# The fourth channel block of a convolutional feed-forward: one product of 128 channels, or four of 32

## The chip, the cores and the metric

The kernel runs on one core of one Trainium2 chip. The metric is the device time of one execution in microseconds (us); runs of the kernel before have a median of 4023.7 us.

## The reference

One block of an image-restoration network, in float32, on `x` of 16 images, 128 channels, 96 x 96 pixels. It is channel attention with a residual, then a feed-forward network with a residual:

```python
xn1 = _layernorm(x_hwc, ln1_w, ln1_b)              # over the 128 channels of a pixel
x = x + _attention(xn1, wq, wk, wv, wp)            # 8 heads; attends between channels, 16 x 16 a head
xn2 = _layernorm(x_hwc, ln2_w, ln2_b)
h1 = jnp.einsum('bchw,oc->bohw', xn2, w_in)        # 128 -> 512 channels, the first projection
h2 = depthwise 3 x 3 convolution of h1 with w_dw   # each of the 512 channels by itself, zeros around
h3 = jax.nn.gelu(h2, approximate=False)
x = x + jnp.einsum('bchw,oc->bohw', h3, w_out)     # 512 -> 128 channels
```

## The kernel before

Channels lie on the 128 partitions and pixels on the free axis. An image is cut into 6 bands of 16 rows (`BR`), so there are 96 bands (`NG`), and the 512 hidden channels into four blocks of 128 (`n` from 0 to 3, the fourth is `PE_CHUNK`). The normalized image lies in `ring`, a buffer of 124 rows that wraps around.

For a band `g` and a block `n`, `conv_job` works in these steps:

- `hidden` (L953): TensorE (PE in the profile) multiplies a chunk of four or five rows, 384 or 480 pixels, by the first projection, into one of four PSUM banks (`H_BANKS`). Where the chunk's rows wrap around in the ring, `pieces` cuts them and there are two products.
- `kept` (L956): ScalarE (ACT) copies the chunk to SBUF and adds the bias.
- `product` (L976) and `add_products` (L990): two of the nine taps of the convolution are made by ScalarE and added by DMAs that GpSimd (POOL) issues.
- `tap` (L983): VectorE (DVE) does the other seven taps, one instruction for each.
- `gelu` (L994): ScalarE applies the activation. Then `ffn_out` (L1083) multiplies by the second projection on TensorE, four rows at a time, four blocks into one bank.

The fourth block has two ways. In some bands (`by_pe(g)`, about three of seven) its projection and its convolution are one set of nine products on TensorE, `by_matmuls` (L1048), and no `conv_job` is made. In the other bands it goes through `conv_job` like the other blocks. A chunk of the fourth block begins two rows later where the band above was a `conv_job` too, as those rows are copied over from it (`halo`).

Around this, TensorE transposes tiles for both normalizations (L695, L781), forms the attention's channel products (L747) and applies the attention's matrix (L644). The attention's small steps are on TensorE in L837 to L919.

The order of all work is made before the program is: `Plan` is a list scheduler with a duration for each operation, four PSUM banks and the other buffers as resources, and a place in line (`AT`, `STEP`) for each kind. The order that it gives is the order on each engine's queue; the hardware only waits where data or a buffer isn't there. `hidden` is handed to it as one operation with the duration `t_mm((e - r) * W)`:

```python
pe(t_mm((e - r) * W), at("hidden", jk, g >= HEAD), lambda r=r, e=e: hidden(r, e), [*zs, ("w", "in")], [ph])
```

Of the kernel before, what the change touches and what calls it, by code (L numbers as in the profile page):

```python
# [21 lines left out]
PE_CHUNK = 3  # L22
# [217 lines left out]
def tile_restormer_block(  # L240
# [24 lines left out]
    nc = tc.nc  # L265
    B, C, H, W = x.shape
    P = 128
# [57 lines left out]
    winT = const.tile([P, NCH, P], F32, name="winT")  # L325
# [26 lines left out]
    def pieces(i, r, n):  # L352

        out, done = [], 0
        while done < n:
            at_ = (i * H + r + done) % RING
            m = min(n - done, RING - at_)
            out.append((done, m, ring[:, at_ : at_ + m, :]))
            done += m
        return out  # L360
# [7 lines left out]
    def rows(t):  # L368
        return t.rearrange("p (r w) -> p r w", w=W)
# [17 lines left out]
    def bank(key, n=4 * P):  # L387

        return banks[plan.slot["h", key]][:, :n]
# [542 lines left out]
    def conv_job(j, g, n):  # L932
# [17 lines left out]
        def hidden(r, e):  # L950
            ph = d["ph", r] = bank((jn, r), (e - r) * W)
            for k, m, z in pieces(i, r0 - 1 + r, e - r):
                nc.tensor.matmul(rows(ph)[:, k : k + m, :], lhsT=winT[:, n, :], rhs=z, start=True, stop=True)  # L953

        def kept(r, e):
            nc.scalar.activation(  # L956
# [44 lines left out]
        for k, (r, e) in enumerate(chunks):  # L1001
            ph = ("h", (jn, r))
            jk, zs = j + STEP["hidden"] * k, z_units(i, r0 - 1 + r, r0 - 1 + e)
            to = [("h1", n, k)]
            if r < 2:
                to.append(("h1", n, "first"))
            if e > BR:
                to.append(("h1", n, "last"))
            pe(t_mm((e - r) * W), at("hidden", jk, g >= HEAD), lambda r=r, e=e: hidden(r, e), [*zs, ("w", "in")], [ph])
            act(t_act((e - r) * W, 1) - 43, at("kept", jk, g >= HEAD), lambda r=r, e=e: kept(r, e), [ph], to)  # L1010
# [177 lines left out]
```

## Time and profile before

| | |
|---|---|
| median of the runs | 4023.7 us (4021.5 to 4025.9) |
| profiled execution, from its first to its last instruction | 4032.2 us |
| instructions | 51,195 |
| PE (products) busy | 3973.7 us, 99% |
| DVE busy | 3964.5 us, 98% |
| ACT busy | 3704.6 us, 92% |
| POOL busy | 1939.2 us, 48% |
| PE weight loads busy | 2593.8 us, 64% |

The profiled execution has no time of its own beside its span, which is 0.2% above the median of the runs. PE's row in the profile counts the products, PEld the weight loads, which run beside them. A line of a group reads: code line, engine, operation, tile written <- tiles read, shapes, number; then busy us, mean ns of one, idle us of the engine ahead of it and what ended that. For a matmul, "128*128" is rows (input channels) by columns (output channels) of the weights, and "128x384" the pixels that pass by. A line of the timeline reads: start, length (both us), engine, line, operation, tiles, shape, number of instructions merged.

### The profile page before, as it was taken

The numbers are of one execution on the slowest core, as the hardware profiler recorded it, in microseconds if no ns is written. First come the engines' busy times: TensorE is split into PE (matmuls) and PEld (weight loads), VectorE is DVE, ScalarE is ACT, GpSimd is POOL, SyncE is SP. The second block draws the span as 40 slices with busy tenths as digits, with TensorE's granted clock in tenths as the row PEclk, the third lists the DMA queues.
The fourth block names the chain that finished last, engine by engine and source line by source line (L and its number), as shares of the span: only waits on it lengthen the run. The fifth ranks groups of instructions, "written<-read, shape, count | busy, mean of one in ns | idle before, by whom it ended". The sixth has DMA issues, their size and how long they took to land.

```text
span 4032.2 us, 51195 instructions
## 1 busy us (share of the span) xinstructions
PE 3973.7 (99%) x17048; PEld 2593.8 (64%) x17048; DVE 3964.5 (98%) x3478; ACT 3704.6 (92%) x7676; POOL 1939.2 (48%) x1596
## 2 busy tenths in 40 slices
PE   9999999999999999999999999999999999999989
PEld 7666666666666666666666666666666666666555
DVE  6999999999999999999999999999999999999999
ACT  7999999899999999999999999999999999999985
POOL 4545445454554544545455454544545455454431
PEclk9999999999999999999999999999999999999999
DMA  5999999999999999999999999999999999999997
GB/s 143 211 202 208 195 218 217 193 230 197 216 220 208 216 203 223 213 209 215 203 215 213 202 216 195 233 206 209 227 196 215 214 219 219 205 214 187 202 192 156
DMA packets 197159, 834.19 MB, mean 207 GB/s; under 512 B 22816, under 2 KB 24352, under 8 KB 196896
## 3 DMA queue, kind: packets, MB, share of 16 engines
q0 software_dynamic: 138960, 679.10, 85.9%
q1 hardware_dynamic: 57936, 151.83, 10.4%
q8 instruction: 136, 2.23, 0.2%
q14 instruction: 127, 1.04, 0.1%
HBM read 150.62 MB, written 149.42 MB: 74 GB/s over the span
## 4 chain that ended last, share of the span: by engine, by line
PE 75%; DVE 11%; ACT 8%; DMA 2%; issue 2%; POOL 2%; POOLq 0%; DVEq 0%; ACTq 0%; SPq 0%
PE h L1083 19%; PE h L1048 19%; PE h L953 16%; DVE h L983 10%; PE g L747 6%; PE h L644 4%; PE pB_a L781 3%; PE pT_a L695 3%; PE pB_b L781 2%; PE pT_b L695 2%; ACT h L976 2%; ACT h L956 1%; POOL rstd_b L713 1%; ACT zT L738 1%; DMA x<-in_x_dram 1%
## 5 line engine op out<-in xcount | busy, mean ns | idle before, releaser
L983 DVE SCALAR_TENSOR_TENSOR h<-h,ratio,h 128x1520 f32<-128x1520 f32 (+1 forms) x1712 | 2983.7, 1778 | 6.5
L1083 PE MATMUL h<-h,woutT 128*128 128x384 f32 x3072 | 1131.9, 488 | 4.1 <-ACT h L956 3.6
L976 ACT ACTIVATE h<-h,ratio 128x1536 f32<-128x1536 f32 (+1 forms) x682 | 1090.3, 1610 | 5.6 <-PE h L1083 3.8
L1048 PE MATMUL h<-xn,comp 128*128 128x380 f32 (+5 forms) x3090 | 1074.7, 478 | 4.4 <-ACT h L956 3.7
L953 PE MATMUL h<-xn,winT 128*128 128x384 f32 (+3 forms) x2720 | 1065.5, 494 | 8.6 <-ACT h L956 4.7
L990 POOL DMA_DIRECT2D h<-h x682 | 628.7, 957 | 885.2 <-ACT h L976 399.5
L956 ACT ACTIVATE h<-h,beta 128x384 f32<-128x384 f32 (+1 forms) x1318 | 791.2, 632 | 76.9 <-PE h L953 54.8
L1083 PEld LDWEIGHTS h<-h,woutT 128*128 128x128 f32 x3072 | 554.2, 190 | 335.0 <-issue 36.7
L1048 PEld LDWEIGHTS h<-xn,comp 128*128 128x128 f32 x3090 | 557.2, 191 | 312.5 <-issue 22.2
L713 POOL TENSOR_TENSOR rstd_a<-ve_a,mhalf 128x4 f32<-128x4 f32 x288 | 527.5, 1844 | 447.1 <-ACT ve_a L709 428.0
L713 POOL TENSOR_TENSOR rstd_b<-ve_b,mhalf 128x4 f32<-128x4 f32 x288 | 564.6, 1986 | 351.4 <-ACT ve_b L709 346.2
L953 PEld LDWEIGHTS h<-xn,winT 128*128 128x128 f32 x2720 | 486.1, 190 | 279.8 <-issue 19.8
L983 DVE SCALAR_TENSOR_TENSOR h<-h,ratio 128x1536 f32<-128x1536 f32 x342 | 618.4, 1810 | 5.9 <-ACT h L956 3.2
L994 ACT ACTIVATE h<-h 128x1536 f32<-128x1536 f32 (+1 forms) x345 | 520.7, 1510 | 23.9 <-DMA h<-h 21.4
L738 ACT ACTIVATE zT<-pT_b,rstd_b 128x128 f32<-128x128 f32 x1132 | 329.6, 403 | 35.4 <-POOL rstd_b L713 33.4
L738 ACT ACTIVATE zT<-pT_a,rstd_a 128x128 f32<-128x128 f32 x1080 | 316.5, 411 | 4.8 <-POOL rstd_a L713 3.7
L747 PEld LDWEIGHTS g<-zT 128*128 128x128 f32 x2160 | 275.0, 191 | 42.8 <-ACT zT L738 0.9
L644 PE MATMUL h<-xn,mwT 128*128 128x384 f32 x768 | 296.2, 490 | 5.5 <-ACT h L1063 2.1
L656 POOL DMA_DIRECT2D x<-in_x_dram x189 | 182.1, 967 | 237.4 <-ACT x L653 166.6
L747 PE MATMUL g<-zT 128*128 128x129 f32 x2160 | 285.5, 274 | 0.3 <-ACT zT L738 0.3
L653 ACT ACTIVATE x<-h,d 128x384 f32<-128x384 f32 x378 | 227.1, 637 | 11.2 <-PE h L644 4.3
L781 PEld LDWEIGHTS pB_b<-ident,zT 128*128 128x128 f32 x1152 | 147.0, 142 | 111.0 <-issue 52.2
(185 smaller groups left out, 3226.3 us busy)
## 6 DMA issues: line engine op xcount, KB each, us to landing
h<-h POOLq DMA_DIRECT2D x569, 768.0 KB, 10.0
h<-h POOLq DMA_DIRECT2D x113, 720.0 KB, 13.2
x<-in_x_dram SPq DMA_DIRECT2D x192, 384.0 KB, 8.2
out_dram<-x SPq DMA_DIRECT2D x190, 384.0 KB, 9.9
x<-in_x_dram POOLq DMA_DIRECT2D x189, 384.0 KB, 10.7
out_dram<-h POOLq DMA_DIRECT2D x94, 768.0 KB, 10.3
out_dram<-x SPq DMA_DIRECT2D x4, 192.0 KB, 1.9
h<-in_L_conv_w_in_dram SPq DMA_DIRECT2D x1, 256.0 KB, 6.3
```

Source lines behind the costliest of these rows:

```text
L644: nc.tensor.matmul(rows(pm), lhsT=mats[i][0], rhs=interior(i, u), start=True, stop=True)
L713: nc.gpsimd.tensor_tensor(rstd, d["ve"], mhalf, ALU.pow)
L738: nc.scalar.activation(zT(q)[:, k, :P], d["pT", q][:, k, :], AF.Copy, scale=d["rstd"][:, t : t + 1])
L747: nc.tensor.matmul(grams[i][:, : P + 1], lhsT=zt[:, :P], rhs=zt, start=(q == 0 and k == 0), stop=(q == NU * TPU // QT - 1 and k == QT - 1),)
L953: nc.tensor.matmul(rows(ph)[:, k : k + m, :], lhsT=winT[:, n, :], rhs=z, start=True, stop=True)
L956: nc.scalar.activation(window(h1_, r, e - r, 1), rows(d.pop(("ph", r))), AF.Identity, bias=beta[:, n : n + 1])
L976: nc.scalar.activation(d["pr", t][:, o0:o1, :], shifted(t, o0, o1), AF.Copy, scale=ratio[:, n, t : t + 1])
L983: nc.vector.scalar_tensor_tensor(h3[:, o0:o1, w0:w1], shifted(t, o0, o1, w0, w1), ratio[:, n, t : t + 1], onto, ALU.mult, ALU.add)
L990: nc.gpsimd.dma_start(out=to[:, o0:o1, :], in_=d["pr", t][:, o0:o1, :], accum_op=ALU.add)
L994: nc.scalar.activation(h3, h3, AF.Gelu)
L1048: nc.tensor.matmul(d["pc"][:, o0 + k : o0 + k + m, w0:w1], lhsT=comp[:, t, :], rhs=z[:, :, w0 + dx : w1 + dx], start=(t == order[0]), stop ...
L1083: nc.tensor.matmul(rows(d["po"]), lhsT=woutT[:, n, :], rhs=h3s[g, n][:, s * UR : (s + 1) * UR, :], start=(k == 0), stop=(k == NCH - 1),)
```

## The change

In the products of `hidden`, where the block is the fourth, the 128 output channels are cut into four slices of 32. Each slice has a product of its own, with 32 columns of the weights, the same pixels, and 32 partitions of the same PSUM bank as its output. Blocks 0 to 2 keep one product. The planner's durations and places are as they were.

```diff
         def hidden(r, e):
             ph = d["ph", r] = bank((jn, r), (e - r) * W)
             for k, m, z in pieces(i, r0 - 1 + r, e - r):
-                nc.tensor.matmul(rows(ph)[:, k : k + m, :], lhsT=winT[:, n, :], rhs=z, start=True, stop=True)
+                parts = [slice(c, c + 32) for c in range(0, P, 32)] if n == PE_CHUNK else [slice(0, P)]
+                for c in parts:
+                    nc.tensor.matmul(
+                        rows(ph)[c, k : k + m, :], lhsT=winT[:, n, c], rhs=z, start=True, stop=True
+                    )
```

## The prediction

> **What bounds the kernel now.** I read the page first (busy shares, slices, the chain), then what TensorE (PE) waits for, then its instructions in order of time, to see how far apart two products start.
>
> ```profile
> PE 3973.7 (99%) x17048; PEld 2593.8 (64%) x17048; DVE 3964.5 (98%) x3478; ACT 3704.6 (92%) x7676; POOL 1939.2 (48%) x1596
> ...
> PE   9999999999999999999999999999999999999989
> ...
> PEclk9999999999999999999999999999999999999999
> ...
> PE 75%; DVE 11%; ACT 8%; DMA 2%; issue 2%; POOL 2%; POOLq 0%; DVEq 0%; ACTq 0%; SPq 0%
> ```
>
> PE is busy in every slice at a full clock and is 75% of the chain. DVE at 98% is nearly as full, ACT at 92% less. A busy PE can hide short stalls, because the recorded end of a product lies behind the start of the next one. So the next view gives PE's idle time, the first two and the last of 26 rows:
>
> ```profile
> PE pB_b L781 <- ACT xn L784: 8.6, 8, 2.7
> PE h L953 <- ACT h L956: 4.7, 7, 2.2
> ...
> PE pB_a L781 <- ACT zT L738: 0.2, 1, 0.2
> ```
>
> The 26 rows add up to 53 us, and 4032.2 - 3973.7 is 58.5 us. What PE could give back by waiting less is at most that. The timeline shows what its busy time consists of:
>
> ```profile
> 1999.72 1.77 PE L953 MATMUL h<-xn,winT 128*128 128x480 f32 x4
> 2001.50 5.43 PE L1083 MATMUL h<-h,woutT 128*128 128x384 f32 x16
> 2006.77 2.73 PE L1048 MATMUL h<-xn,comp 128*128 128x384 f32 x8
> 2009.33 0.60 PE L695 MATMUL pT_b<-ident,x 128*128 128x128 f32 x4
> ```
>
> and the groups, each shape apart, how many there are:
>
> ```profile
> L1083 PE MATMUL h<-h,woutT 128*128 128x384 f32 x3072 | 1131.9, 488 | 4.1 <-ACT h L956 3.6 <-ACT h L994 0.3
> ...
> L953 PE MATMUL h<-xn,winT 128*128 128x384 f32 x2060 | 800.4, 488 | 6.8 <-ACT h L956 4.3 <-ACT x L653 1.0 <-ACT h L1063 0.8
> L1048 PE MATMUL h<-xn,comp 128*128 128x380 f32 x1916 | 720.4, 484 | 0.0
> ...
> L983 DVE SCALAR_TENSOR_TENSOR h<-h,ratio 128x1536 f32<-128x1536 f32 x342 | 618.4, 1810 | 5.9 <-ACT h L956 3.2 <-PE h L1083 2.1 <-ACT zT L738 0.6
> ...
> L1048 PE MATMUL h<-xn,comp 128*128 128x384 f32 x958 | 391.7, 491 | 4.4 <-ACT h L956 3.7 <-ACT h L1063 0.8
> ...
> L644 PE MATMUL h<-xn,mwT 128*128 128x384 f32 x768 | 296.2, 490 | 5.5 <-ACT h L1063 2.1 <-ACT x L653 1.7 <-ACT h L956 1.2
> L747 PE MATMUL g<-zT 128*128 128x129 f32 x2160 | 285.5, 274 | 0.3 <-ACT zT L738 0.3
> ...
> L953 PE MATMUL h<-xn,winT 128*128 128x480 f32 x508 | 241.2, 567 | 1.2 <-ACT x L653 0.8 <-ACT h L956 0.4
> ...
> L781 PE MATMUL pB_b<-ident,zT 128*128 128x128 f32 x1152 | 191.3, 275 | 9.8 <-ACT xn L784 8.6 <-ACT zT L738 1.0
> ...
> L781 PE MATMUL pB_a<-ident,zT 128*128 128x128 f32 x1080 | 177.7, 273 | 0.2 <-ACT zT L738 0.2
> ...
> L695 PE MATMUL pT_b<-ident,x 128*128 128x128 f32 x1132 | 169.8, 274 | 5.1 <-ACT zT L738 2.5 <-DMA x<-in_x_dram 2.4
> L695 PE MATMUL pT_a<-ident,x 128*128 128x128 f32 x1080 | 162.3, 273 | 2.0 <-ACT zT L738 2.0
> ```
>
> Eight records of 384 columns last 2.73 us together and one lasts 0.491, so they start (2.73 - 0.49) / 7 = 0.320 us apart, not 0.49. In the same way records of 480 columns are (1.77 - 0.567) / 3 = 0.401 us apart, those of 128 (0.60 - 0.274) / 3 = 0.109. L1083 has 96 bands x 4 steps x 4 blocks = 1536 products in the code and 3072 records: one f32 product is two records, each with a weight load, so 384 columns cost 0.64 us. Now PE's real work: 6858 records of 384 columns at 0.320 (2195 us), 508 of 480 at 0.401 (204), 1916 of 380 at 0.317 (607), 2160 of 129 and 4444 of 128 at 0.109 (720), together 3726 us, 92% of the span, without the smaller groups. **PE is full with streaming, not with waiting.** Time added to it lengthens the span nearly one for one.
>
> **What the change adds.** It removes nothing and moves nothing: `STEP`, `AT` and the planned durations are untouched, so the order on each engine stays, on the DMA queues too. Only the products of block 3 in bands whose conv is not on PE change. There are 342 conv jobs (the L983 row of 1536 columns is the first tap of each) less 288 for blocks 0 to 2, so 54 such bands. By the code they have 214 chunks, and with the ring's wraps 220 products: 142 of 384 columns, 71 of 480, six of 96, one of 288. Their streaming today is 2 x (142 x 0.320 + 71 x 0.401 + 6 x 0.080 + 0.240) = 149 us, the last two scaled by columns from 0.320. After the change there are 880 products, 660 more, or 1320 more records and as many loads, each of the same moving columns onto 32 partitions. What they cost is not in this trace, but its nearest rows are products with a single output channel (128*1), in the attention step:
>
> ```profile
> 1969.25 0.84 PE L1083 MATMUL h<-h,woutT 128*128 128x384 f32 x2
> 1969.93 0.59 PE L837 MATMUL g<-wqkT,gs 128*128 128x256 f32 x2
> 1970.45 0.38 PE L838 MATMUL g<-wqkT,gs 128*1 128x128 f32 x2
> 1970.67 0.38 PE L840 MATMUL g<-wqkT,gs 128*1 128x128 f32 x2
> 1970.98 0.55 PE L781 MATMUL pB_a<-ident,zT 128*128 128x128 f32 x3
> 1971.36 0.81 PE L1083 MATMUL h<-h,woutT 128*128 128x384 f32 x2
> ```
>
> *Term 1, a narrow product's own time.* L838 and L840 start 0.22 us apart, two records of 0.11: one output channel takes as long as 128 (0.109). A product of 32 channels therefore takes 0.64 us at 384 columns too, and cutting by channels returns nothing. These four records go to the same output partition, one after another; the trace has no narrow products for different partitions side by side, and so doesn't show whether the four can run at once. Bounds: all in turn, eight record times in place of two, adds 3 x 149 = 447 us; all four at once adds 0. Between them lies the case that follows from the order alone. Each product is a pair of records that follow each other on the same 32 channels, and in all rows records start in program order. If different groups of channels can overlap, the second record of a group still waits for the first, and the next group's first one stands behind it in the queue: group 2 starts with the second record of group 1, group 3 with the second of group 2. That is five record times in place of two, so 1.5 x 149 = 224 us. I take this one, with both ends kept for the range: the next paragraph shows that narrow products do run in another mode than wide ones, which the first end ignores, and the start in program order, which the other end ignores, is in every row. The Trainium skill speaks on two sides of this. "TensorE: Matmul & The Clock Gate" (Part 3, "What overlaps and what doesn't") says that products on different tiles of the array overlap, and that products nevertheless start and end strictly in program order; by that rule term 1 is the 224 us. The skill's "TensorEngine Tiling (Array Packing)" (Theoretical Speedup) gives up to 4x for a dimension of at most 32, by which term 1 would be near 0. No row here shows such an overlap.
>
> *Term 2, going into the narrow mode and out.* The last record of L837 starts 0.215 us behind 1969.93 (256 columns at 0.320/384) and would be streamed at 1970.36; L838 starts at 1970.45, 0.09 late, with no wait named. Behind the last record of L840, L781 could start at 1970.67 + 0.22 = 1970.89 and starts at 1970.98, again 0.09 late, and then its own three records take 0.38 to the next group where 3 x 0.109 = 0.33 is usual: the weights of 128 columns could not be loaded ahead, 0.05 here. For a product of 384 columns the same exposed load is what makes the 16 records of L1083 above last 5.43 us and not 15 x 0.320 + 0.49 = 5.29, so up to 0.14. The load of the first 32 columns going in is between nothing and the 0.14 of 128 columns; I take 0.03, in proportion. One chunk so pays 0.09 + 0.03 + 0.09 + 0.05 to 0.14 = 0.26 to 0.35 us, and 214 chunks pay 56 to 75 us if each stands alone between wide products. Some follow each other, so I take 60. Within a chunk I count no further change, as L838 to L840 show none. The Trainium skill, "TensorEngine Tiling (Array Packing)" (Key Properties), says that a change of the tiling mode drains the engine and a change of the tile alone doesn't; the 0.09 agrees with the first half, and no row here shows the second.
>
> *Term 3, what comes back.* The evictions and everything behind them only start later:
>
> ```profile
> L956 ACT ACTIVATE h<-h,beta 128x384 f32<-128x384 f32 (+1 forms) x1318 | 791.2, 632 | 76.9 <-PE h L953 54.8
> ```
>
> ACT takes 0.63 us for a chunk, and behind a late one stand in its queue the products, scalings and copies of the next steps, which PE needs later still; PE's next product goes to another of the four banks and doesn't wait for this chunk's eviction. So the whole line shifts and I count no new wait of PE; DVE, at 98%, is let off. Some of PE's 53 us of waits close while the others catch up: between 0 and 53, I take 22. The cost is not covered by anything, as PE has no other idle time. Sum: 224 + 60 - 22 = 262 us on the span of 4032.2, 6.5%. The timed runs had a median of 4023.7, 8.5 us under that span, and I put the sum on the median: **4286 us**.
>
> **Rivals.**
> - *All in turn*, four groups that never overlap: 447 + 60 - 26 = 481 us, so 4505. For it: L838 and L840, the only narrow neighbours, do run in turn. Against it: they go to one and the same partition, where nothing else was possible. Without the mode change it would be some 4445.
> - *All four at once*: term 1 is 0, 60 - 10 = 50 us remain, 4074, which is not slower by 2%. The place is PE's queue: it decides if a group's first record may start while the record ahead of it still waits for its own group. For it: a wait of one part need not hold another part. Against it: no row shows a record that started ahead of an earlier one. If eight pairs of load and product can't follow each other closer than the 0.109 us of the L695 row, the chunk takes 0.87 and not 0.64 us, 49 us more in 214, so 4123.
> - *Worse than in turn*, each product paying its own way in and out (880 x 0.3 = 264 in place of 60): 4709. Against it: L838 to L840 cost nothing extra.
> - *Faster*: there is nothing that the change takes off any engine; only luck with the waits.
>
> **How the numbers follow.** Five record times 0.42 (own range 4250 to 4323, from 53 to 0 us returned and 56 to 75 for the mode), all in turn 0.38, all at once 0.17, worse 0.02, faster 0.01. The range takes in the first two, with all in turn up to 447 + 75 above the median: 4250 to 4546 holds 0.80. About 2% (80 us) is what a measurement of this kernel tells from no change. Faster by that: 0.01; within it: 0.16, all at once without the bound on issue; slower: 0.83.
>
> **What would show it.** L953 gets a form 128*32 with 880 x 2 records, of which the 384-column ones start in program order. In five-times form a chunk's eight records span 5 x 0.32 = 1.6 us from first start to last streamed, and the starts come in close pairs; in turn they are 0.32 apart, 2.56 us; at once all lie within 0.1 to 0.35 us of each other in pairs. Ahead of and behind a chunk stand 0.09 us. DVE's share falls to about 92% and ACT's to 86% with their busy us unchanged; DVE's idle time goes to waits for L956. I am wrong in the mechanism if the records are evenly spaced, and wrong in term 3 if the span grows by over 60 us more than PE's records do.

## The result, and the profile after

The changed kernel takes 4075.7 us where the kernel before takes 4023.7, a ratio of 1.0131 (1.0102 to 1.0161). Timed again with more runs it is 4074.6 against 4022.5, **1.0129 (1.0112 to 1.0146)**: 52 us slower, clear of the noise but under the bound of 2%, so by that bound no change. The forecast was 4286 with a range of 4250 to 4546. The result is the rival *all four at once*, which was put at 4074 and given 0.17.

The page of the changed kernel, the lines that answer to those of before (busy us, share of the span, instructions; then PE's clock in slices, and the chain):

```profile
PE 4022.3 (99%) x18368; PEld 2535.4 (62%) x18368; DVE 3972.1 (98%) x3478; ACT 3719.1 (91%) x7676; POOL 1884.9 (46%) x1596
...
PEclk9999999999999999999999999999999999999999
...
PE 81%; ACT 9%; DVE 4%; issue 3%; POOL 2%; DMA 1%; POOLq 0%; DVEq 0%; ACTq 0%
```

The 1320 records that the change adds are there (18368 - 17048), and 1320 loads with them. The chain has become more PE's (75% to 81%), DVE's part went from 11% to 4%. DVE is at 98% as before and ACT at 91% (92% before), since the span is hardly longer.

The groups of the first projection, each shape apart:

```profile
L955 PE MATMUL h<-xn,winT 128*128 128x384 f32 x1776 | 686.7, 487 | 5.4 <-ACT h L960 3.7 <-ACT x L653 1.0 <-ACT h L1067 0.5
...
L955 PE MATMUL h<-xn,winT 128*32 128x384 f32 x1136 | 119.1, 496 | 0.6 <-ACT h L960 0.4 <-ACT h L1097 0.3
L955 PE MATMUL h<-xn,winT 128*32 128x480 f32 x568 | 71.6, 577 | 0.2 <-ACT h L960 0.2
```

This is the line that gives the case away. The 1136 narrow records of 384 columns last 496 ns each by their records, like the wide ones (487), but the engine was busy with them for 119.1 us only: 0.105 us for each, against 0.387 for a wide one (686.7 / 1776). Where records run at the same time, a record's own length doesn't say what it costs; the busy time of its group over its count comes nearer. Some four of them are under way at a time.

The timeline around one chunk of block 3, and one stretch of it (us from the span's start; length; PE busy with the records in it, and how many; the same of the loads; then the granted clock, and the DMAs' share and GB/s):

```profile
2091.99 0.80 PE L1052 MATMUL h<-xn,comp 128*128 128x380 f32 x2
2092.72 0.85 PE L955 MATMUL h<-xn,winT 128*32 128x384 f32 x8
2093.50 0.91 PE L1052 MATMUL h<-xn,comp 128*128 128x384 f32 x2
```

```profile
2092.72:2093.04 0.32, 0.32 (x4) 0.16 (x8) 1.00 1.41 281
```

Eight narrow records of 384 columns take 0.78 us from the first start to the next wide one (2093.50 - 2092.72), where two wide ones take 0.64. In the first 0.32 us, one record time, four records run and all eight loads are made. The second four start 0.35 us behind the first. So it is at all 189 places where PE comes to such products: the first four records start within 20 ns. The trace doesn't name a record's group. That the first four are the first record of each group follows from the first run below, where records on one group run one at a time. In the program the two records of a group stand together, group after group, so **the first record of group 1 started ahead of the second record of group 0, which stands before it**. The planner's order is the order on PE's queue, but here PE doesn't start its records in that order. Ahead of the chunk, the two 380-column records from 2091.99 on could be streamed at 2092.62; the chunk starts 0.10 later. Behind it, L1052's two records last 0.91 us where two last 0.81, the exposed load.

PE's waits, the first two rows of 25:

```profile
PE pB_b L781 <- ACT xn L784: 6.5, 6, 2.3
PE h L955 <- ACT h L960: 4.5, 6, 2.3
...
```

They add up to 44 us, 9 less than before. No wait that is new among them is longer than 0.8 us in all.

### The profile page after: what moved, and what is told of

Same layout as the page of the kernel before. It is cut to its first block, busy times and chain, and to the rows that moved or that the text cites. A ratio compares the mean times of both kernels' runs of the same rounds, so it can differ in the third digit from the quotient of the medians.

```text
span 4071.0 us, 53836 instructions
## 1 busy us (share of the span) xinstructions
PE 4022.3 (99%) x18368; PEld 2535.4 (62%) x18368; DVE 3972.1 (98%) x3478; ACT 3719.1 (91%) x7676; POOL 1884.9 (46%) x1596
## 4 chain that ended last, share of the span: by engine, by line
PE 81%; ACT 9%; DVE 4%; issue 3%; POOL 2%; DMA 1%; POOLq 0%; DVEq 0%; ACTq 0%
PE h L1087 21%; PE h L1052 20%; PE h L955 18%; PE g L747 6%; PE h L644 4%; DVE h L987 3%; PE pB_a L781 3%; PE pT_a L695 3%; PE pB_b L781 3%; PE pT_b L695 2%; ACT h L980 2%; ACT h L960 1%; ACT zT L738 1%; ACT h L998 1%; POOL rstd_b L713 1%
## 5 line engine op out<-in xcount | busy, mean ns | idle before, releaser
L1087 PE MATMUL h<-h,woutT 128*128 128x384 f32 x3072 | 1135.3, 489 | 4.8 <-ACT h L960 3.4
L1052 PE MATMUL h<-xn,comp 128*128 128x380 f32 (+5 forms) x3090 | 1081.1, 480 | 3.6 <-ACT h L960 2.8
L955 PE MATMUL h<-xn,winT 128*128 128x384 f32 (+5 forms) x4040 | 1073.3, 502 | 8.2 <-ACT h L960 4.5
L994 POOL DMA_DIRECT2D h<-h x682 | 644.4, 980 | 893.9 <-ACT h L980 433.3
L1087 PEld LDWEIGHTS h<-h,woutT 128*128 128x128 f32 x3072 | 550.1, 190 | 351.5 <-issue 54.8
L1052 PEld LDWEIGHTS h<-xn,comp 128*128 128x128 f32 x3090 | 550.7, 191 | 336.3 <-issue 52.6
L713 POOL TENSOR_TENSOR rstd_a<-ve_a,mhalf 128x4 f32<-128x4 f32 x288 | 507.5, 1768 | 478.0 <-ACT ve_a L709 453.2
L713 POOL TENSOR_TENSOR rstd_b<-ve_b,mhalf 128x4 f32<-128x4 f32 x288 | 530.8, 1872 | 376.6 <-ACT ve_b L709 368.5
L955 PEld LDWEIGHTS h<-xn,winT 128*128 128x128 f32 (+1 forms) x4040 | 443.9, 154 | 329.3 <-issue 84.0
L747 PEld LDWEIGHTS g<-zT 128*128 128x128 f32 x2160 | 274.3, 191 | 45.6 <-issue 5.2
L747 PE MATMUL g<-zT 128*128 128x129 f32 x2160 | 286.3, 275 | 0.3 <-ACT zT L738 0.3
L702 DVE BATCH_NORM_STATS2 st_b<-pT_b 128x6 f32<-128x256 f32 x566 | 212.6, 419 | 20.8 <-PE pT_b L695 19.5
```

The source lines that it names most:

```text
L713: nc.gpsimd.tensor_tensor(rstd, d["ve"], mhalf, ALU.pow)
L747: nc.tensor.matmul(grams[i][:, : P + 1], lhsT=zt[:, :P], rhs=zt, start=(q == 0 and k == 0), stop=(q == NU * TPU // QT - 1 and k == QT - 1),)
L955: nc.tensor.matmul(rows(ph)[c, k : k + m, :], lhsT=winT[:, n, c], rhs=z, start=True, stop=True)
L994: nc.gpsimd.dma_start(out=to[:, o0:o1, :], in_=d["pr", t][:, o0:o1, :], accum_op=ALU.add)
L1052: nc.tensor.matmul(d["pc"][:, o0 + k : o0 + k + m, w0:w1], lhsT=comp[:, t, :], rhs=z[:, :, w0 + dx : w1 + dx], start=(t == order[0]), stop ...
L1087: nc.tensor.matmul(rows(d["po"]), lhsT=woutT[:, n, :], rhs=h3s[g, n][:, s * UR : (s + 1) * UR, :], start=(k == 0), stop=(k == NCH - 1),)
```

## The experiments

The theory after the result, A: records for different groups of 32 columns run at the same time, whatever their order in the program, and the 52 us are the way into the narrow mode and out. The rivals: a narrow record is cheap by itself (B); the groups share something, and the 52 us are the price of sharing; records wait in a common line, and the change just got by.

**All four on one group.** Same number of records, same mode, no other group; channels 32 to 127 of the block are left out:

```diff
-parts = [slice(c, c + 32) for c in range(0, P, 32)] if n == PE_CHUNK else [slice(0, P)]
+parts = [slice(0, 32)] * 4 if n == PE_CHUNK else [slice(0, P)]
```

> All four products of a chunk of block 3 take the same 32 channels and write the same 32 partitions (channels 32 to 127 of that block are left out). Same number of records, same mode, one group of columns. Theory A (products on different groups of columns run at once, those on one group in turn): eight record times a chunk in place of two, 3 x 149 = 447 us on top of the changed kernel's 4076, less some 20 to 40 of waits: 4480 to 4525. Theory B (a product of 32 columns is simply short, or pipelined, whatever its group): no change, 4066 to 4086.

Measured 4515.1 us, 489 over the kernel before. Its groups, the first 0.33 us of a chunk, and the timeline around this chunk and the next:

```profile
L955 PE MATMUL h<-xn,winT 128*32 128x384 f32 x1136 | 391.2, 489 | 0.0
L955 PE MATMUL h<-xn,winT 128*32 128x480 f32 x568 | 241.6, 569 | 0.2 <-ACT h L960 0.2
```

```profile
1530.14:1530.47 0.33, 0.33 (x1) 0.13 (x2) 1.00 0.82 168
```

```profile
1529.40 0.81 PE L1087 MATMUL h<-h,woutT 128*128 128x384 f32 x2
1530.14 5.99 PE L955 MATMUL h<-xn,winT 128*32 128x384 f32 x16
1536.06 0.49 PE L747 MATMUL g<-zT 128*128 128x129 f32 x2
```

The same 1136 records now keep the engine busy for 391.2 us and not 119.1, and one runs at a time. A is right, B is out: the records are not cheap, they share the time because they are on different groups. The price of the narrow mode is there too, though nothing is shared: L1087's records could be streamed at 1530.04 and the chunk starts 0.10 later; its 16 records need 8 x 0.322 + 8 x 0.4025 + 0.03 for the first load = 5.83 us, so they could be streamed at 1535.97, and L747 starts 0.09 later. This run is also the rival *all in turn* of the prediction, put at 4505.

**Each product twice, a group's two together (c0 c0 c1 c1 c2 c2 c3 c3), or round the groups (c0 c1 c2 c3 c0 c1 c2 c3).** The second product writes the same values again:

```diff
+parts = [p for p in parts for _ in range(2 if n == PE_CHUNK else 1)]
```

```diff
+parts = parts * (2 if n == PE_CHUNK else 1)
```

> Each of the four products is issued twice, both of a group before the next group (c0 c0 c1 c1 c2 c2 c3 c3); the second writes the same values again. Theory A1 (each group has its own line, and a waiting record holds up nobody else's): the four groups still run at once with four records each, four record times in place of two, +149 us on 4076, less up to 20 of waits: 4205 to 4230. Theory A2 (one record may wait for its group, but a second one waiting for the same group stops all behind it): a group starts only when the group before it is at its third record, ten record times in place of two, +8 x 75 = 597 us: 4640 to 4680.

> The same eight products as in the blocked order, but round the groups (c0 c1 c2 c3 c0 c1 c2 c3). Both A1 and A2 give four record times in place of two: 4205 to 4230. If it comes out well above this, records of different groups slow each other down when more of them are in flight.

Measured 4229.2 and 4222.2 us. Both are at four record times in place of two. The 7 us between the two single runs are no more than the runs of the kernel before beside them differ (4025.1 to 4031.8). The blocked order, first 0.33 us and first 1.31 us of a chunk:

```profile
1441.35:1441.68 0.33, 0.33 (x4) 0.17 (x8) 1.00 0.48 93
1441.35:1442.66 1.31, 1.31 (x16) 0.58 (x17) 1.00 0.87 169
```

Four run from the start though three more records of group 0 stand ahead of group 1, and all 16 are through in 1.31 us, four times 0.33. So up to three waiting records of a group don't hold up the next group, and A2 (a second waiting record stops all behind it) is out.

**Each product eight times, then three times, blocked.** The same edit with 8 and with 3.

> As in the blocked order of two, but each product eight times (16 records and 16 loads of group 0, then those of group 1, and so on: 128 instructions for a chunk's piece). If a group's waiting records never hold up the next group: sixteen record times in place of two, 14 x 75 = 1044 us on 4076, some 5120, and the first records of the four groups start within some 0.2 us. If the engine looks ahead over a limited number of instructions (64 would be two groups here), groups 2 and 3 start only as records of groups 0 and 1 finish, and a chunk takes 17 to 32 record times: 5200 to 6300.

Measured 7806.2 us, beyond both cases: the waiting is not unlimited, and a bound on the number of instructions as it was put there doesn't give this time either. Four stretches of one chunk, 64 records of 480 columns, 0.40 us each:

```profile
2985.21:2990.06 4.85, 4.85 (x12) 1.34 (x13) 1.00 0.51 105
2990.06:2994.92 4.86, 4.86 (x17) 1.41 (x16) 1.00 1.07 216
2994.92:2999.79 4.87, 4.87 (x19) 1.42 (x18) 1.00 0.81 203
2999.79:3006.20 6.41, 6.41 (x21) 1.74 (x19) 1.00 0.00 0
```

In the first 4.85 us there are 12 records, one at a time (12 x 0.40 = 4.82): only group 0 runs. By the order of starts in the trace, group 1 comes in 6 ns behind group 0's 13th record, when one of its 16 is running and three are waiting, and the same repeats for groups 2 and 3. That makes 3 x 12 + 16 = 52 record times. That is 50 more than the changed kernel's two, which take 149 us or 74.6 each: 50 x 74.6 = 3730 us on 4076, or 7806. That a single run hits this to the microsecond is luck, as neighbouring chunks share some time and the waits change too. So the theory was put anew: each group takes one running and three waiting records, and a fifth stops all that stand behind it. It was tested on three times, six records of a group:

> Each product three times in blocked order: six records of a group before the next group. With eight times, group 1 started when group 0 was at its 13th of 16 records, that is with one running and three waiting. If a group takes just four records before it stops the queue: group 1 starts with group 0's third record, group 2 with group 1's third, so 3 x 2 + 6 = 12 record times in place of two, +10 x 75 = 746 us on 4076, less up to 40 of waits: 4780 to 4830. If the bound is on the number of instructions looked ahead and not on a group's records (48 of them stand in a chunk's piece here): six record times, +299 us, 4355 to 4385.

Measured 4797.9 us, within the case of four. Two stretches from the start of a chunk of 384 columns:

```profile
1619.96:1620.62 0.66, 0.66 (x2) 0.24 (x3) 1.00 1.48 233
1619.96:1623.90 3.94, 3.94 (x29) 1.79 (x31) 1.00 1.02 159
```

Group 0 is alone for two record times, as six records less four ask for, and the whole chunk takes 3.94 us, 12 times 0.33. (Of the 29 records in this stretch 24 are the chunk's; five of the next chunk have begun.)

**The mode alone.** The kernel before, with a product of 32 channels and one pixel ahead of each wide product of block 3, which writes over it:

```diff
+if n == PE_CHUNK:
+    nc.tensor.matmul(
+        rows(ph)[:32, k : k + 1, :1], lhsT=winT[:, n, :32], rhs=z[:, :1, :1], start=True, stop=True
+    )
 nc.tensor.matmul(rows(ph)[:, k : k + m, :], lhsT=winT[:, n, :], rhs=z, start=True, stop=True)
```

> The kernel before, one product of 128 channels, with one tiny product of 32 channels and one pixel ahead of each product of block 3 (the wide product overwrites it). So the way into the narrow mode and out is there and the four-way product is not. Theory S (the whole 52 us are the change of mode: 0.095 in, 0.03 load, 0.094 out, 0.06 to 0.11 exposed load for 189 stretches): 64 us of PE and some 10 for the tiny products, less 10 to 25 of waits, 4065 to 4090, ratio to before 1.010 to 1.016. Rival (the cost is that four products run at once, sharing the pixels' path): 4024 to 4040, ratio under 1.004.

Measured 4085.4 us, ratio 1.0144 (1.0127 to 1.0161): 60 us, with no four-way product at all. The timeline of one, where L954 is the tiny product and L957 the wide one:

```profile
1217.99 0.49 PE L781 MATMUL pB_a<-ident,zT 128*128 128x128 f32 x3
1218.41 0.22 PE L954 MATMUL h<-xn,winT 128*32 128x1 f32 x2
1218.56 0.91 PE L957 MATMUL h<-xn,winT 128*128 128x384 f32 x2
1219.31 1.13 PE L1052 MATMUL h<-xn,comp 128*128 128x384 f32 x3
```

Three transposes from 1217.99 are streamed at 1218.32, and the tiny product starts 0.09 later. The wide one starts 0.15 behind it and its two records take 0.75 us to the next group in place of 0.64. That is 0.35 us for a product that computes nothing of use, as much as the four-way products pay at a place (0.34, below). There are 220 tiny products, each by itself, against 189 places, and 220 x 0.35 = 77 us on PE, of which 60 came out at the end. The tiny product's own time is within the 0.15; the run with all four on one group pays the same 0.10 and 0.09 us without it. So the price is the mode's, not the sharing's.

**Two products of 64 channels.**

```diff
-parts = [slice(c, c + 32) for c in range(0, P, 32)] if n == PE_CHUNK else [slice(0, P)]
+parts = [slice(c, c + 64) for c in range(0, P, 64)] if n == PE_CHUNK else [slice(0, P)]
```

> Two products of 64 channels in place of four of 32. If the 52 us are the way into the mode and out, once per stretch: as the changed kernel, with the first load 0.05 in place of 0.03 us and a shorter stagger: 4070 to 4085. If each product has a price of its own: half, 4040 to 4055.

Measured 4079.4 us in a single run, 51 over the kernel before beside it (4028.4), and within the first case: half the products, the same price.

**All four blocks cut.**

```diff
-parts = [slice(c, c + 32) for c in range(0, P, 32)] if n == PE_CHUNK else [slice(0, P)]
+parts = [slice(c, c + 32) for c in range(0, P, 32)]
```

> The four-way products for all four blocks of channels (1360 products become 5440). In the kernel before, the records of L953 stand in 1010 separate stretches on PE, against 189 of block 3. If the price is 0.34 us a stretch (less 0.05 where a transpose follows): 1010 x 0.33 = 333 us, less 20 to 50 of waits: 4310 to 4345. If it is a price for each chunk's product (1360 x 0.34 = 462): 4440 to 4480.

Measured 4306.4 us, 4 under the first case and far from the second. PE's starts give 344 us over the streaming for the 1010 stretches, 0.34 each: 99 ahead of them, 150 within, 94 behind. 278 reached the end. The 66 us between are not all waits that closed elsewhere: at the same 1010 places the kernel before already lost some 37 us over the streaming by its starts. PE's rows of waits add up to 29 us here, 24 less than before.

**The planner told.** The duration of block 3's chunks 340 ns longer, so that the order of all engines is made with it:

```diff
-pe(t_mm((e - r) * W), at("hidden", jk, g >= HEAD), ...
+pe(t_mm((e - r) * W) + (340 if n == PE_CHUNK else 0), at("hidden", jk, g >= HEAD), ...
```

> The changed kernel with the planner's duration of block 3's chunks 340 ns longer, as the trace shows it; the order of all engines is made anew. PE's own 64 us stay. If the 52 us are PE's time and nothing else: 4060 to 4095, no gain that a measurement can tell. If part of it is an order that no longer fits: down to 4040.

Measured 4078.2 us, ratio 1.0126 (1.0103 to 1.0149). No gain: the 52 us are PE's time, and this new order found no place to put it.

**The change once more.**

> The changed kernel once more, timed against the kernel before on one chip, for a narrower interval: 1.010 to 1.016 as before; the account of PE's records (64 us more on PE, 10 to 25 us of waits closed) asks for 39 to 54 us, 1.0097 to 1.0134.

Measured 4074.6 us, ratio 1.0129 (1.0112 to 1.0146), 52 us.

No run points to a version that beats the kernel before: four groups at once do in one record time what the whole array does in one.

## Why the prediction was wrong

- **What bounds the kernel** was right. PE has no room: time added to PE came out at the end, in the four-way kernel (64 us on PE, 52 at the end), with all blocks cut (344, 278) and in turn (489 at the end).
- **Term 1 failed**, 224 us forecast, 0 measured: a chunk's eight records take two record times, as one product of 128 channels does, and not five. The narrow product's own time was right: 0.32 us a record at 384 columns. In turn on one group was right too: the run with all four on one group came to 4515, and the rival *all in turn* was put at 4505. What failed is the step from "in all rows records start in program order" to "the next group's first record stands behind a waiting one". Those rows could not show it. In the kernel before, all records between two changes of mode use one and the same group, or the whole array, so nothing in it could have passed anything. I used rows without the choice as evidence on the choice, and so gave the case that was measured 0.17. The rule that speaks for program order, in "TensorE: Matmul & The Clock Gate" of the Trainium skill (Part 3, "What overlaps and what doesn't"), holds here for the overlap of tiles and not for the strict order of starts: four groups start within 20 ns, ahead of second records that stand before them, and the measurement decides. The drain that the Trainium skill, "TensorEngine Tiling (Array Packing)" (Key Properties), puts on a change of mode, and not on a change of tile, agrees with the runs in both halves: 0.09 us going in and out, and 7 ns from one group to the next.
- **Term 2 was right**, 60 us forecast, 64 measured by PE's starts: 189 stretches with 0.097 us ahead (18 us), 0.149 more within than the streaming (28 us: the first load 0.03, the way out 0.09, four staggered starts 0.02), and 0.11 or 0.06 of exposed load behind (18 us). The 0.02 was not in the forecast. The tiny products alone cost as much at a place.
- **Term 3**: in the rival I let 10 us of waits close. 64 - 52 = 12, so the 4074 was hit to 2 us because two terms, 4 and 2 us too small, partly cancel. At the same 189 places the kernel before already lost some 9 us over the streaming, so most of the 12 need not be waits elsewhere. The two profiled spans alone would say 25 (4071.0 - 4032.2 = 38.8), but before's was 8.5 us over the median of its runs.
- **Bound on issue**, 49 us more if pairs of load and product can't follow each other within 0.109 us: not so. Eight loads were made in 0.16 us of the 0.32 above, and the four groups' first records start 7 ns apart.

## What to carry to other kernels

Before a case in the middle is chosen between "in turn" and "at once", ask if any row could have come out otherwise; where none could, they give no reason to prefer the middle to the ends. Products on different groups of output columns run together on this engine for the price of one, as long as no group has more than three records waiting. So cutting a product costs only the change of mode, some 0.34 us for each stretch of narrow products among wide ones; a full array gains nothing by it. A product of few channels that stands alone between wide ones pays that price as well, even with a single pixel, so such products belong next to each other.

## What the runs showed of the hardware

- Records for different column groups overtake each other. With one running and three waiting records of a group the next group still starts; the fifth stops the queue (eight times: 7806 us; three times: 4798).
- Four groups at once stream the same pixels at full rate: a second record of 384 columns follows the first of its group by 0.35 us, of which 0.03 is the group's first load, as on one group alone.
- Products of 64 columns pay the same price for the mode as products of 32: 51 and 52 us over the kernel before.
- The first record of a group behind a change of mode is longer by its load: 510 ns for 32 columns, 537 for 64 and 590 for 128, against 486 for a later one, all with 384 pixels.
